# A graph layer's software pipeline re-cut: 46 steps per tile instead of 43, its small operations dealt out anew, its searches spread out

## The chip, the cores and the metric

One core of a Trainium2 chip. The metric is the device time of the whole kernel in microseconds (us). The core has a matmul engine (PE, whose weight loads stand in the profile as PEld), a vector engine (DVE), an activation engine (ACT), a general engine (POOL, which also issues indirect DMAs) and SP, which only issues DMAs. Each engine runs its own instructions in order; they meet at semaphores.

## The reference

Two graph layers run one after the other on 3327 nodes with 256 features. Layer 0 is graph attention followed by a GRU cell. The adjacency has about 4 neighbours per row.

```python
Wh = h @ W;  src = Wh @ a[:F];  dst = Wh @ a[F:]
e   = leaky_relu(src + dst.T, 0.2)
att = softmax(where(adj > 0, e, -9e15), axis=1)
gi  = (att @ Wh) @ w_ih.T + b_ih;   gh = h @ w_hh.T + b_hh
r, z = sigmoid(i_r + h_r), sigmoid(i_z + h_z);  n = tanh(i_n + r * h_n)
x = layernorm(x + (1 - z) * n + z * h)
# layer 1: two propagation steps (sparse mean, and top-p attention over all nodes),
# a sum of projections, layer norm, residual, layer norm
```

The change touches layer 0 alone.

## The kernel before

The 3327 rows are 26 tiles of 128 rows (the last has 127). Layer 0 has three kinds of work.

*Projection* (`project`, lines 743 to 759). For each tile PE transposes x (`px`), ACT copies it to `xT`, PE multiplies it with W (`pw`), ACT copies the result to one of six `table` buffers, POOL takes two columns from it (`ds`), and a DMA from ACT's queue writes it to `whx` in DRAM, from where all tiles' neighbour rows are gathered later. No gather can start before the whole of `whx` is written.

*Search* (`neighbours`, lines 809 to 828). The adjacency tile (1.66 MB, one of three buffers) comes by `load_adj` on SP's queue. DVE finds the ones in each of four segments (L814, FIND_INDEX8) and sorts the finds into a list of up to 16 neighbours (L819 to L827). These are five steps; `find()` makes one of them. At the end of a search, the load of the tile three further on is issued into the buffer that has come free.

*Tile* (`tile`, lines 830 to 1003). From the list of neighbours come the 640 edge places of the tile: `deg`, `d16`, `pst`, `half`, `square`, `mid`, `first`, `y`, `mem`, `pe`, `ei`, then `edge`, then five gathers of 128 rows from `whx` into `g` (L609, POOL). The weights of the edges are `e` (DVE) and its exponential (ACT). Five 128x128 matrices `m` carry each edge's weight in the column of its row: two are made on ACT (Square, then Relu), two on POOL and one on DVE (L936). PE multiplies them with `g` into `acc` (L942). The rest is the GRU: `prz` and `pn` get their x part (L954, L955), `h` is `acc` scaled, `ph` and `hT` turn it, L967 and L971 add its part, and `rz`, `n`, `x1`, the layer norm (`mv`, `shift`, POOL) and the q and k rows of layer 1 (`qk`) follow.

A tile is a generator, and `yield from to(s)` moves it on to its step s. The order on PE, ACT, DVE and POOL is the order in which the program issues (a manual schedule); SP's DMAs only follow their semaphores. `advance()` is one phase: it makes one `find()`, opens a new tile in every sixth phase, moves each open tile on by one step, oldest first, and moves on the first logits of layer 1, which begin when the last search is done.

```python
            find()
            if phase % EVERY == 0 and phase // EVERY < NT:
                tiles.append(self.tile(phase // EVERY))
            for g in list(tiles):
                if next(g, True):
```

With six phases per tile, a tile that is at step s stands beside others at steps s-6, s-12 and so on, and each engine has in a phase the work of all steps that are equal modulo 6. In the projection loop `find()` is called for each tile from the third on, and from tile 13 (`EARLY`) on each projected tile also makes a phase. Buffers that bind tiles together: three of `g`, ten of `m`, one PSUM bank each of `acc` and `prz`, two of `pn`, and two each of the tags `sm` (`pst`, `pe`, `pq`) and `tr` (`ph`, `ptq`, first logits).

## Time and profile before

| | us |
|---|---|
| median of three runs (lowest to highest) | 1891.27 (1889.89 to 1893.18) |
| profiled execution, its own time | 1886.47 |
| its span, first to last instruction | 1884.5 |
| last copy of the projection (L757) starts | 66.93 |
| first gather / fifth gather of tile 0 (L609) starts | 71.56 / 78.57 |
| fifth gather of tile 25 starts | 393.30 |
| last copy of layer 0 (L639) starts | 428.1 |

| engine | busy us over the span | share |
|---|---|---|
| PE | 1665.2 | 88% |
| PEld | 1223.3 | 65% |
| DVE | 1335.0 | 71% |
| POOL | 1174.2 | 62% |
| ACT | 997.8 | 53% |

The shares are means over stages with different limits. Layer 0 is the first 428 us of the span, the rest is layer 1. In the profile an engine's wait stands in brackets as "[idle before <-releaser]"; "issue" is an idle stretch in which the engine waited for nothing that the profile shows. The granted PE clock is either 1.0 or 0.5, and a mean over a window lies between.

### The profile page before, as it was taken

The page shows a single profiled execution, that of the slowest core. Times are in us where ns is not written, and L with a number is a line of the kernel's source. Part 1 is how long each engine was busy: PE and PEld are TensorE (multiplying, and loading weights), DVE is VectorE, ACT ScalarE, POOL GpSimd, SP SyncE. Part 2 cuts the span into 40 slices and gives each one's busy share as a digit, 9 for nine tenths or more (in the row PEclk, how much of TensorE's full clock was granted, in tenths as well). Part 3 has the DMA queues.
Part 4 walks back from the last instruction along what each step waited for, and adds up shares of the span by engine and source line. Part 5 has one row for each costly group of instructions (what it writes and reads, how often), then busy time and mean ns, then how long its engine had stood idle before and what let it go on. Part 6 is the DMA issues. An engine that isn't in the chain of part 4 may idle for free. (4 is left out here: it accounts for less than half of the span.)

```text
span 1884.5 us, 27520 instructions
## 1 busy us (share of the span) xinstructions
PE 1665.2 (88%) x8093; PEld 1223.3 (65%) x8093; DVE 1335.0 (71%) x4278; ACT 997.8 (53%) x2243; POOL 1174.2 (62%) x1881
## 2 busy tenths in 40 slices
PE   6578888987999999999996999999999988679994
PEld 4345455545677777777774777777777665568873
DVE  6789886446555566655564999999999977485872
ACT  3244445554556555555653555555555446676663
POOL 1477778847787666666654666655666573555764
PEclk9789889997999999999998999999999998889997
DMA  9766652213222111111101111111111110122330
GB/s 330 255 208 230 216 169 64 62 43 86 84 67 57 40 40 41 47 47 45 40 26 39 51 54 48 49 45 48 54 57 54 48 54 29 40 76 87 118 95 29
DMA packets 95482, 154.21 MB, mean 82 GB/s; under 512 B 16854, under 2 KB 68557, under 8 KB 95324
## 3 DMA queue, kind: packets, MB, share of 16 engines
q1 hardware_dynamic: 64906, 89.92, 14.5%
q0 software_dynamic: 20384, 53.28, 10.7%
q10 hardware_dynamic: 10034, 9.18, 1.5%
q8 instruction: 66, 1.08, 0.2%
q14 instruction: 92, 0.75, 0.1%
HBM read 124.65 MB, written 27.75 MB: 81 GB/s over the span
## 5 line engine op out<-in xcount | busy, mean ns | idle before, releaser
L1416 PE MATMUL pav<-xa,at 128*128 128x256 f32 (+2 forms) x1352 | 331.7, 390 | 9.0 <-ACT at L1402 8.8
L1416 PE MATMUL pav<-x,at 128*128 128x256 f32 (+2 forms) x1352 | 325.7, 385 | 7.6 <-ACT at L1402 7.6
L1402 ACT COPY at<-pt 128x512 f32<-128x512 f32 (+2 forms) x364 | 191.8, 541 | 261.8 <-PE pt L1400 260.5
L1416 PEld LDWEIGHTS pav<-xa,at 128*128 128x128 f32 (+2 forms) x1352 | 246.4, 191 | 90.0 <-ACT at L1402 43.1
L1416 PEld LDWEIGHTS pav<-x,at 128*128 128x128 f32 (+2 forms) x1352 | 244.4, 190 | 72.4 <-ACT at L1402 29.9
L1196 ACT COPY array<-pl 128x416 f32<-128x416 f32 (+4 forms) x405 | 183.2, 503 | 180.3 <-PE pl L1193 180.2
L1209 DVE MAX8 cand<-array 128x8 f32<-128x167 f32 (+5 forms) x921 | 239.0, 335 | 44.7 <-ACT array L1196 44.6
L609 POOL DMA_INDIRECT g<-xf_rows,edge x130 | 136.3, 1049 | 158.0 <-PE pxf L1362 125.6
L609 POOL DMA_INDIRECT g<-x_rows,edge x130 | 140.3, 1079 | 104.4 <-PE ptq L622 71.3
L1193 PE MATMUL pl<-kT,qT 64*128 64x416 f32 (+4 forms) x810 | 198.1, 560 | 4.5 <-ACT x L1581 2.7
L1301 DVE TENSOR_TENSOR_SCAN before<-e 128x40 f32<-128x40 f32 (+3 forms) x52 | 14.9, 286 | 225.5 <-ACT e L1294 225.5
L1354 POOL TENSOR_SCALAR m<-col,erow 128x128 f32<-128x128 f32 x260 | 162.6, 639 | 14.5 <-PE pxf L1362 8.0
L609 POOL DMA_INDIRECT g<-whx,edge x130 | 137.4, 1057 | 46.4 <-issue 32.1
L1362 PE MATMUL pxf<-g,m 128*128 128x256 f32 (+1 forms) x520 | 133.5, 406 | 15.3 <-POOL m L1354 8.6
L1362 PEld LDWEIGHTS pxf<-g,m 128*128 128x128 f32 (+1 forms) x520 | 99.0, 199 | 69.8 <-issue 41.3
L1227 DVE MAX8 lst<-cand 128x8 f32<-128x160 f32 (+3 forms) x364 | 114.6, 315 | 9.0
L1400 PE MATMUL pt<-ident,array 128*128 128x128 f32 (+1 forms) x676 | 100.9, 276 | 7.1 <-DVE array L1317 7.1
L814 DVE FIND_INDEX8 at<-ones,array 128x8 uint32<-128x840 f32 (+1 forms) x104 | 106.5, 1026 | 0.0
L1400 PE MATMUL pt<-ident,p 128*128 128x128 f32 (+2 forms) x676 | 100.2, 274 | 3.9 <-DVE p L1317 3.9
L1400 PEld LDWEIGHTS pt<-ident,array 128*128 128x128 f32 (+1 forms) x676 | 84.8, 144 | 24.8 <-PE pxf L1362 7.9
L967 PE MATMUL prz<-wih,hT 128*128 128x512 f32 (+1 forms) x104 | 67.0, 778 | 36.9 <-ACT hT L965 36.9
L1400 PEld LDWEIGHTS pt<-ident,p 128*128 128x128 f32 (+2 forms) x676 | 84.5, 144 | 21.3 <-PE pxf L1362 7.7
(473 smaller groups left out, 3369.4 us busy)
## 6 DMA issues: line engine op xcount, KB each, us to landing
array<-in_adj_dram SPq DMA_DIRECT2D x25, 1248.0 KB, 7.0
array<-in_adj_dram SPq DMA_DIRECT2D x25, 415.5 KB, 6.2
xf_rows<-xf SPq DMA_DIRECT2D x50, 128.0 KB, 1.7
xa_rows<-xa SPq DMA_DIRECT2D x50, 128.0 KB, 1.7
xfs<-xf_rows SPq DMA_DIRECT2D x50, 128.0 KB, 2.4
whx<-table ACTq DMA_DIRECT2D x25, 129.5 KB, 6.2
x_rows<-x ACTq DMA_DIRECT2D x25, 128.0 KB, 2.4
xb_rows<-xb SPq DMA_DIRECT2D x25, 128.0 KB, 1.7
```

Of the source, the lines that this page charges most:

```text
L609: self.nc.gpsimd.indirect_dma_start(out=dst[:, b, :], out_offset=None, in_=table[:, :], in_offset=bass.IndirectOffsetOnAxis(ap=self.edge[: ...
L814: nc.vector.max_index(at[:r, g, :], self.ones8[:r], ad[:r, g, :])
L967: nc.tensor.matmul(prz[:r], hT[:, c, :r], self.wih[:, c, : 2 * D], start=False, stop=(c == DC - 1))
L1193: nc.tensor.matmul(pl[:r, :w], q[on], self.sh.kT[on, n, s : s + w], start=True, stop=True)
L1196: nc.scalar.copy(l[:r, h * HALF + s : h * HALF + s + w], pl[:r, :w])
L1209: self.nc.vector.max(cand[:r, g * 8 : g * 8 + 8], src[:r, g * group : min(N, (g + 1) * group)])
L1227: nc.vector.max(lst[:r, k : k + 8], cand[:r])
L1354: nc.gpsimd.tensor_scalar(v.m[:, b, :], sh.col1, sh.erow[:, v.at, b : b + 1], None, ALU.is_equal)
L1362: nc.tensor.matmul(acc[:r, :D], v.m[:, b, :r], v.g[:, b, :], start=(b == 0), stop=(b == EB - 1))
L1400: nc.tensor.transpose(pt[: rows(j), j - j0, :r], v.p[:r, cols(j)], self.ident[:r, :r])
L1402: nc.scalar.copy(at[:, :full, :r], pt[:, :full, :r])
L1416: nc.tensor.matmul(v.acc[: v.r, :D], at[:k, j - 4 * g, : v.r], V[:k, j, :], start=(j == 0), stop=(j == NT - 1))
```

## The change

Step numbers are new throughout; a tile has 46 steps instead of 43, still six phases per tile. Where a result went from one engine to the next in the same step or in the next one, there is now mostly a step or two between. `e` is made at step 22 after gathers at 14 to 17 (before: 18, after 13 to 15); `hT` is at 31 and its matmuls at 33 and 34 (before: both at 28); the x part of `pn` is at 29 and that of `prz` at 30.

Between engines: `d1`, `d16`, the floor of `info` and `edge` go from DVE to POOL; `mid` and `first` go from DVE to ACT, `y` stays on ACT and comes two steps earlier; all five `m` are made on ACT by a Square and an Exp with the weight as its bias, so that POOL's two and DVE's one, `we`, `wm` and `minus` go; `most` is a second row of `e`.

Searches: in the projection loop `find()` is called from tile 5 on and in two of three phases (16 calls instead of 24), then once per phase up to phase 23, then five times in six phases. Only adjacency tile 0 is loaded at the start; tiles 1 and 2 are loaded from ACT's queue after projected tiles 4 and 10, and the two GRU weights after tiles 15 and 17 (before: both after 6). `a` is laid out by the host so that each partition reads 16 bytes in a row.

```diff
+FINDS = (0, 0, 0, 2, 1, 2)
+FAR = 10000.0
...
         if apart:
             yield
+            yield
         for half in (on, other):
...
-        nc.scalar.dma_start(self.a_sb, a.rearrange("(c p) o -> p (c o)", p=P))
+        nc.scalar.dma_start(self.a_sb, a)
...
-        nc.vector.tensor_scalar(info[:r, 0:1], info[:r, 0:1], 1.0, None, ALU.max)
+        yield from to(1)
+        d1 = self.small("d1", f"d1_{t}")
...
+        nc.gpsimd.tensor_scalar(d1[:r], deg[:r], 1.0, None, ALU.max)
         d16 = self.small("d16", f"d16_{t}", dtype=BF16)
-        nc.vector.tensor_scalar(d16[:r], deg[:r], 1.0, None, ALU.max)
+        nc.gpsimd.tensor_copy(d16, d1)
+        nc.gpsimd.tensor_scalar(info[:r, 0:1], info[:r, 0:1], 1.0, None, ALU.max)
         yield from to(2)
...
-        nc.gpsimd.tensor_copy(d1, d16)
...
         yield from to(4)
-        nc.vector.tensor_scalar(mid, pst[:, 0:1], -1.0, half, ALU.mult, ALU.add)
-        nc.vector.tensor_copy(first, pst[:, 0:1])
-        yield from to(6)
+        nc.scalar.activation(mid, pst[:, 0:1], AF.Identity, bias=half, scale=-1.0)
+        nc.scalar.copy(first, pst[:, 0:1])
         y = self.work.tile([P, EB * P], F32, tag="y", name=f"y{t}", bufs=1)
         nc.scalar.activation(y, self.place, AF.Square, bias=mid)
+        yield from to(6)
...
-        nc.vector.tensor_scalar(sh.edge[:, t, :], k, -1.0, float(N + 1), ALU.mult, ALU.add)
-        yield from to(13)
-        sh.gather(g, sh.whx, t, (0, 1))
-        yield from to(14)
-        sh.gather(g, sh.whx, t, (2, 3))
-        yield from to(15)
+        yield from to(14)
+        nc.gpsimd.tensor_scalar(sh.edge[:, t, :], k, -1.0, float(N + 1), ALU.mult, ALU.add)
+        sh.gather(g, sh.whx, t, (0,))
+        yield from to(15)
+        sh.gather(g, sh.whx, t, (1,))
+        yield from to(16)
+        sh.gather(g, sh.whx, t, (2, 3))
+        yield from to(17)
         sh.gather(g, sh.whx, t, (4,))
...
-        for k in (3, 4):
-            nc.scalar.activation(ms[k], sh.col1, AF.Square, bias=minus[:, k : k + 1])
-        yield from to(18)
+        for step, ks in ((20, (0, 1)), (21, (2, 3, 4))):
+            yield from to(step)
+            for k in ks:
+                nc.scalar.activation(ms[k], sh.col1, AF.Square, bias=self.erow(t)[:, k : k + 1], scale=-1.0)
+        yield from to(22)
...
-            nc.scalar.activation(ms[k], ms[k], AF.Relu, scale=v[:, k : k + 1], bias=w[:, k : k + 1])
-        yield from to(21)
-        for k in (0, 1, 2):
-            (nc.vector if k == 0 else nc.gpsimd).tensor_scalar(
-                ms[k], sh.col1, self.erow(t)[:, k : k + 1], w[:, k : k + 1], ALU.is_equal, ALU.mult
-            )
-        yield from to(24)
+        for step, ks in ((23, (0, 1)), (24, (2, 3)), (25, (4,))):
+            yield from to(step)
+            for k in ks:
+                nc.scalar.activation(ms[k], ms[k], AF.Exp, bias=e[:, 0, k : k + 1], scale=-FAR)
+        yield from to(26)
         acc = self.ps1.tile([P, 512], F32, tag="acc", name=f"acc{t}")
...
-        yield from to(25)
+        yield from to(28)
         rs = self.small("rs", f"rs{t}")
...
-        prz = self.ps1.tile([P, 2 * D], F32, tag="prz", name=f"prz{t}")
+        yield from to(29)
+        h = self.work.tile([P, D], F32, tag="h", name=f"h{t}")
+        nc.scalar.activation(h[:r], acc[:r, :D], AF.Copy, scale=rs[:r])
         pn = self.ps.tile([P, 2 * D], F32, tag="pn", name=f"pn{t}")
         ones3 = self.ones3[:, :r]
+        nc.tensor.matmul(pn[:r], ones3, self.bias[:, 2 * D :], start=True, stop=False)
+        xs = [self.xT[:, c, cols(t)] for c in range(DC)]
+        for c in range(DC):
+            nc.tensor.matmul(pn[:r, :D], xs[c], self.whh[:, c, 2 * D :], start=False, stop=False)
+        yield from to(30)
+        prz = self.ps1.tile([P, 2 * D], F32, tag="prz", name=f"prz{t}")
         nc.tensor.matmul(prz[:r], ones3, self.bias[:, : 2 * D], start=True, stop=False)
-        nc.tensor.matmul(pn[:r], ones3, self.bias[:, 2 * D :], start=True, stop=False)
...
-        yield from to(28)
+        yield from to(31)
         hT = self.work.tile([P, DC, P], F32, tag="hT", name=f"hT{t}")
         nc.scalar.copy(hT[:, :, :r], ph[:, :, :r])
+        yield from to(33)
...
+        yield from to(34)
...
-        yield from to(29)
+        yield from to(35)
 
         rz = self.work.tile([P, 2 * D], F32, tag="rz", name=f"rz{t}")
         nc.scalar.activation(rz[:r], prz[:r], AF.Tanh, scale=0.5)
-        yield from to(32)
+        yield from to(36)
...
-        yield from to(33)
+        yield from to(37)
         nc.scalar.activation(n[:r], n[:r], AF.Tanh)
-        yield from to(35)
+        yield from to(38)
...
-        yield from to(37)
+        yield from to(39)
...
-        yield from to(38)
+        yield from to(40)
         nc.scalar.activation(x1, x1, AF.Identity, bias=shift[:r], scale=mv[:r, 1:2])
         move_rows(nc.scalar, sh.x1_rows[t * P : t * P + r, :], x1, r)
-        yield from to(39)
+        yield from to(41)
         yield from sh.qk(self.ps, self.work, 0, t, x1, "tr")
...
-        for t in range(3):
-            self.load_adj(t)
+        self.load_adj(0, nc.sync)
-        cuts = (0, 8, 16, 23, NT)
+        cuts = (0, 8, 16, NT - 2, NT)
...
-                if t == 6:
-                    for w, src in zip((self.whh, self.wih), self.gates):
-                        nc.scalar.dma_start(w, src.rearrange("(c p) d -> p c d", p=P))
+                if t in (4, 10):
+                    self.load_adj(1 + t // 10, nc.scalar)
+                if t in (15, 17):
+                    w, src = ((self.whh, self.wih)[t // 17], self.gates[t // 17])
+                    nc.scalar.dma_start(w, src.rearrange("(c p) d -> p c d", p=P))
...
-                    advance()
-                elif t >= 2:
+                    advance(min(1, phase % 3))
+                elif t >= EARLY - 8:
                     find()
...
             while phase < EVERY * NT or tiles:
-                advance()
+                advance(1 if phase < 4 * EVERY else FINDS[phase % EVERY])
```

## The prediction

> **What bounds the kernel now.** Only layer 0 changes, and there the page's slices show no engine at nine tenths throughout. I therefore cut the span into stretches first, and then read what each engine waits for, and one engine's timeline.
>
> Busy time by stretch, for ten tiles (tiles 7 to 16 open at 133.4 and 266.6) and for one tile:
>
> ```profile
> core 0: us, PE busy (x) PEld busy (x) DVE busy (x) ACT busy (x) POOL busy (x), PEclk, DMA share, GB/s
> 133.40:266.60 133.20, 109.15 (x479) 67.75 (x478) 113.51 (x429) 61.46 (x190) 101.13 (x192) 0.91 0.67 216
> ```
> ```profile
> 290.15:302.25 12.10, 9.90 (x46) 6.03 (x45) 9.71 (x43) 6.71 (x22) 9.90 (x20) 1.00 0.26 67
> ```
>
> Ten tiles take 133.2 us, 13.3 each, where an undisturbed tile takes 12.1. By busy time PE, DVE and POOL are level and all about a fifth idle. The timeline of POOL over that tile says otherwise:
>
> ```profile
> 290.15 1.14 POOL L609 DMA_INDIRECT g<-whx,edge  x1 [0.52 <-PE acc L942]
> 291.59 1.00 POOL L609 DMA_INDIRECT g<-whx,edge  x1 [0.30 <-issue]
> ...
> 295.20 0.19 POOL L859 CAST d<-d 128x1 f32<-128x1 bf16 x1
> 295.49 0.18 POOL L862 TENSOR_SCALAR half<-d 128x1 f32<-128x1 f32 x1
> 295.65 0.26 POOL L864 TENSOR_SCALAR square<-d 128x1 f32<-128x1 f32 x1
> 295.85 0.19 POOL L865 CAST tell<-info 128x16 bf16<-128x16 f32 x1
> 296.13 0.25 POOL L866 TENSOR_TENSOR tell<-info,tell 128x16 bf16<-128x16 f32 x1
> 296.37 1.60 POOL L936 TENSOR_SCALAR m<-col,erow,we 128x128 f32<-128x128 f32 x2
> 298.13 1.32 POOL L609 DMA_INDIRECT g<-whx,edge  x1 [0.17 <-issue]
> ...
> 301.47 0.26 POOL L998 TENSOR_SCALAR shift<-mv 128x1 f32<-128x1 f32 x1
> 302.25 1.13 POOL L609 DMA_INDIRECT g<-whx,edge  x1 [0.52 <-PE acc L942]
> ```
>
> There is no real wait in it. Every gather carries a gap of 0.30 after another gather, 0.17 after `m` and about 0.5 after a small operation, whichever releaser is named; the small ones stand 0.16 to 0.29 apart although they last 0.19. POOL is full: 12.1 us is its own work. The fifth gather of tile 0 starts at 78.57, that of tile 25 at 393.30: 25 intervals of 12.59. So POOL's work makes 12.1 of it and waits the rest. From the waits at 120 to 290 us (total, times, longest):
>
> ```profile
> PEld prz L967 <- ACT hT L965: 24.6, 13, 2.7
> DVE e L922 <- DMA g<-whx,edge: 15.7, 5, 5.2
> POOL g L609 <- issue: 15.0, 54, 0.5
> POOL mv L995 <- DVE which L894: 10.2, 6, 2.0
> ```
>
> POOL's one true wait is `mv`, 2 us in about every second tile: DVE sits in `e` for a gather that has not landed (landing takes 2.7 to 9.0 us, while adjacency loads keep the DMA share at 0.67), makes up its queue, and reaches the layer norm late. PE's wait for `hT`, 1.9 per tile, is beside POOL's chain.
>
> The projection (to 66.93) is another regime. Its waits:
>
> ```profile
> PE pa L737 <- DMA a_sb<-in_a_dram: 9.9, 1, 9.9
> DVE at L814 <- DMA array<-in_adj_dram: 9.6, 3, 6.1
> ACT xT L749 <- DMA whx<-table: 4.9, 2, 2.8
> ```
>
> The DMA share is 0.95 over the first 70 us (327 GB/s): x, the rows of `whx`, the GRU weights and eight adjacency tiles compete.
>
> **The sum for before**, in trace time: 67 projection, 11.6 to tile 0's fifth gather, 314.7 for 25 intervals, 34.8 from there to the end of layer 0 at 428, and 1456.4 of layer 1: 1884.5. The profiled execution has 1886.5 with what lies around the span; the median of the runs is 1891.3, 4.8 above. I put savings to the median as they come out.
>
> **Part 1, POOL's period.** Out: both `m`, 296.37 to 298.13, 1.76. The lone gather then follows a small operation instead of `m`: +0.33. The cast of `d` goes, -0.29; `d1`, `d16` and the floor of `info` come, by the spacing of `half`, `square`, `tell`: 0.28+0.28+0.18 = +0.74. `edge` comes with an output in uint32 that POOL shows nowhere: between 0.16 (the spacing of a small operation) and 0.5, taken at 0.25, as DVE needs 0.17 for it and POOL 0.21 to 0.32 for other 128x5 operations. New period 12.10-1.76+0.33-0.29+0.74+0.25 = 11.37, that is -0.73, over 25 intervals **-18**.
>
> A rule speaks against this move: the Trainium skill, "GPSIMD Engine Reference", section "Engine selection", wants elementwise work on VectorE[...]. The rows: `d` on DVE lasts 0.146, a cast of the same size on POOL 0.19 to 0.22, but what counts on a full POOL is its spacing.[...] I keep the rows.
>
> **Part 2, POOL's waits.** The 25 intervals exceed 12.1 by more than 0.5 each; the first two (10.7, 11.0) and last two (10.8, 10.5) are short of work, so the other 21 carry 271.7-254.1 = 17.6 of waiting. `e` is now five steps behind the last gather instead of three: at 1.9 us per step 9.5 us instead of 6.3, at the upper end of landing. I keep a quarter of the wait: **-13**. What is late next: `edge` (step 14) and `mv` (39) wait for DVE one step earlier. DVE's work per tile is 11.35 with 1.2 searches; 0.2 of a search less (a segment search is 1.03, the sort about 1, so 5.1 each) is -1.0, and `info`, `d16`, `mid`, `first`, `edge`, `most` and one `m` (0.15+0.15+0.20+0.15+0.17+0.16+0.33) is -1.3: 9.0. It has room of 2.4.
>
> **Part 3, ACT and PE.** ACT loses two Square, two Relu, `we`, `wm`, `minus` (6.8+8.8 over 20 each: 1.5, plus 0.6), gains five Square and five Exp, `mid` and `first`. Exp with a bias column has no row of this size; Square with one is 0.386, Relu with two 0.486, both are the bounds, I take 0.386: 3.9+0.35. 6.15 rises to about 8.3, under 11.4: cost nothing, covered by POOL. If that cover went, ACT would be due at 8.6, the `x_rows` issue of 0.33 included. Moved past ACT's queue is also `mid`, which waits for POOL's `half`; behind it stand `y`, `rz`, `h`. PE's `hT` stall goes (two steps lie between), which leaves 9.9 per tile: no gain in time, as POOL holds the period. Its only effect is on the clock, which was 0.91 here; at 10 of 11.4 it should be nearer 1.
>
> **Part 4, projection.** In a clean stretch (19.51, 20.60, 21.93, 23.02) a tile costs ACT 1.17: 26 make 30.4 from 12.3. Before, 0.9 of weight issues and 1.5 of tile work come to it: 45, so 22 of the 67 are stalls. Afterwards: start about 2 earlier, as `a` comes in 128 runs instead of 512 (between 0 and 3.6: it takes 8.0 to land, the bigger W2 4.4); four adjacency issues on ACT's queue, each like the GRU weights' 0.4 to 0.5, +1.8; two tiles' `mid`, `first`, +1.5. SP's queue is relieved of four issues. Stalls: adjacency traffic falls from eight loads to about six, 3.3 MB, at 395 GB/s 8 us; DVE, in whose queue the searches stood, makes 16 instead of 24, and its 9.6 us on `array` mostly go. On the other side, writes of `whx` now queue behind 1.66 MB on the same queue, twice 4 us, with six `table` buffers (7 us) to absorb it. I take 9 of stalls left of 22. Sum -2+1.8+1.5-13 = about **-12**, between -21 and 0.
>
> **Part 5, the end.** After the last gather there are 28 steps instead of 27 at 1.29 each: **+1.5**. The last search ends near phase 148 instead of 119; first logits still end with the last tile, since their chunks wait for finished tiles: 0. Layer 1 is untouched: 0.
>
> **Sum**: -18-13-12+1.5 = -41.5. Smaller POOL contention (the cast took 0.45 once beside a DVE search) and the last intervals, from which 0.74 more goes, add about -3. Forecast 1891-45 = **1846**.
>
> **The rivals.**
> R1, POOL is not the bound, busy time is right. The skill's "Perfetto Trace Analysis", section "Identifying the Most-Contended Engine", takes occupancy for GPSIMD and LDWEIGHTS busy time for TensorE. By it POOL's 9.9 of 12.1 has room, LDWEIGHTS has 6.0, and with the stall at `hT` gone the period falls to PE's 9.9 plus hops, 10.3: -57-12+1.5, 1824. The gapless timeline speaks against it, the unexplained gaps "issue" for it. Chance 0.13.
> R2, new waits in the place of the old: the period stays at 12.1 (ACT's `x` and `mid` wait for POOL, and `rz`, which frees the single `prz` bank, stands behind). -12-12+1.5: 1869. The 17.6 us of waits show that such loops exist; the longer distances speak against. Chance 0.18.
> R3, the projection gains nothing, as its writes stand behind adjacency loads in one queue: 1858. Chance 0.06.
> R4, slower. The one mechanism: ACT blocked at `mid` or `x` behind a full POOL holds `rz`, PE stops at `prz` long enough each tile for its clock to fall, and PE becomes the bound. It decides from a mean interval of 12.59+12/25 = 13.1 on; with 1 us of idle PE that needs 9.9 of work at a clock of 0.82. At 13.6 the sum is +25-12 = +13, 1904. The window 133 to 267 had 0.91 at 13.3, so it is not absurd; chance 0.05.
> The forecast keeps 0.58. The kernel does what it says in the order of its instructions, so nothing is kept for that.
>
> **How the numbers follow.** The forecast's own range is 1832 to 1860 (stalls of the projection 9 either way, `edge` 7, waits 6). To leave out no more than two in ten the range must take in R1 and R2: 1820 to 1870. This kernel's runs spread so that about 0.2% (3.8 us) can be told from no change. Faster 0.94 (all but R4 and a sliver of R2), same 0.01, slower 0.05.
>
> **What would show it.** Right: POOL in mid layer 0 without a true wait and with 11.2 to 11.6 between fifth gathers; no `mv` wait; `e` not waiting for `g`; PE without the wait for `hT`; last copy of the projection at 50 to 58; layer 0 over at about 383. Wrong: POOL waiting for DVE or ACT in every tile (R2), a period under 11 (R1), a clock below 0.85 in mid layer 0 (R4).

## The result and the profile after

The kernel after takes 1860.93 us (median; 1859.89 to 1862.4), the kernel before in the same session 1890.62: ratio 0.984, interval 0.9824 to 0.9858, 29.7 us. Its profiled execution has 1861.15 with a span of 1859.1. The forecast was 1846, in a range of 1820 to 1870: faster, as said, but with two thirds of the gain. Set beside the terms of the prediction, in trace time:

| term | before | after | predicted change | measured |
|---|---|---|---|---|
| start of tile 0's fifth gather | 78.57 | 76.17 | -12 | -2.4 |
| the 25 intervals between fifth gathers | 314.7 | 284.9 | -34 | -29.8 |
| last fifth gather to the end of layer 0 | 34.8 | 38.7 | +1.5 | +3.9 |
| layer 1 | 1456.4 | 1459.3 | 0 | +2.9 |

The sum is -25.4 (1884.5 to 1859.1); the profiled execution before was some 4 us quicker than the median of its runs, which is the rest. Layer 1 isn't touched by the change; in the profiled executions of this study it took from 1453 to 1464, so below the stages of layer 0 are compared in the traces, and whole times by their ratios to the kernel before, with intervals.

The windows of the kernel after, ten tiles and one tile (from fifth gather to fifth gather), in the columns of the rows of before:

```profile
128.44:245.86 117.42, 107.26 (x470) 65.36 (x468) 98.51 (x330) 74.41 (x241) 94.78 (x201) 0.91 0.65 214
199.30:211.05 11.75, 11.75 (x47) 7.34 (x47) 9.96 (x33) 7.46 (x26) 9.46 (x20) 0.79 0.67 212
```

Ten tiles in 117.4 where there were 133.2, and each takes 11.7 or 11.8: the irregular intervals (12 to 15 us) have gone. PE's clock is 0.91 as before. In the one tile PE shows busy throughout, at a clock of 0.79, and ten tiles have it busy for nine tenths: that PE is the bound is a rival to be tested below. POOL's timeline over the same tile:

```profile
199.30 1.01 POOL L613 DMA_INDIRECT g<-whx,edge  x1 [0.30 <-issue]
200.33 0.21 POOL L918 TENSOR_TENSOR src<-ei 128x5 f32<-128x5 f32 x1
200.65 0.76 POOL L921 TENSOR_SCALAR e<-src,dmax 128x5 f32<-128x5 f32 x1
201.38 0.43 POOL L880 CAST tell<-info 128x1 bf16<-128x1 f32 x1
201.89 0.19 POOL L881 TENSOR_TENSOR tell<-info,tell 128x1 bf16<-128x1 f32 x1
202.05 0.23 POOL L858 TENSOR_SCALAR d<-deg 128x1 f32<-128x1 f32 x1
202.34 0.19 POOL L860 CAST d<-d 128x1 bf16<-128x1 f32 x1
202.49 0.21 POOL L862 TENSOR_SCALAR info<-info 128x1 f32<-128x1 f32 x1
202.78 0.20 POOL L908 TENSOR_SCALAR edge<-k 128x5 uint32<-128x5 f32 x1
203.26 1.15 POOL L613 DMA_INDIRECT g<-whx,edge  x1 [0.28 <-POOL edge L908]
...
207.01 1.11 POOL L613 DMA_INDIRECT g<-whx,edge  x1 [0.43 <-issue]
...
211.05 1.01 POOL L613 DMA_INDIRECT g<-whx,edge  x1 [0.31 <-issue]
```

Again no true wait. `d`, its cast and the floor of `info` take 0.73 from start to start (202.05 to 202.78; forecast 0.74). What the forecast didn't have is in two rows: `e`'s second row with 0.76, where the same addition as `most` lasted 0.32 before, and the cast of `tell` with 0.43, 0.18 before. The two in the undisturbed tile of before:

```profile
299.81 0.32 POOL L915 TENSOR_SCALAR most<-src,dmax 128x5 f32<-128x5 f32 x1
300.08 0.18 POOL L874 CAST tell<-info 128x1 bf16<-128x1 f32 x1
```

DVE in the tile of after, at that moment:

```profile
200.42 0.55 DVE L884 TENSOR_SCALAR mem<-y,square 128x640 bf16<-128x640 f32 x1
200.88 0.42 DVE L989 SCALAR_TENSOR_TENSOR n<-rz,n 128x256 f32<-128x256 f32 x1
201.33 0.42 DVE L990 TENSOR_TENSOR x<-x,n 128x256 f32<-128x256 f32 x1
```

POOL's `e` starts beside `mem` and ends 0.11 after the end of `n`; the cast of `tell` starts beside `x` and ends 0.06 after it. And the waits at 120 to 290 us (total, times, longest):

```profile
ACT x L1001 <- POOL shift L999: 40.2, 15, 3.6
POOL g L613 <- issue: 18.8, 57, 0.4
...
ACT hT L964 <- PE ph L961: 14.5, 10, 3.2
```

The three true waits of before (`prz` for `hT`, `e` for `g`, `mv` for DVE) are gone; POOL's only entries are the gaps ahead of its gathers. ACT now waits for POOL's `shift`, some 2.7 us in nearly every tile, at its instruction `x`; nothing that POOL needs comes late by it, as POOL has no wait.

### The profile page after: what moved, and what is told of

Read it like the earlier page. It is cut to its first block, busy times and chain, and to the rows that moved or that the text cites. A ratio compares the mean times of both kernels' runs of the same rounds, so it can differ in the third digit from the quotient of the medians.

```text
span 1859.1 us, 27521 instructions
## 1 busy us (share of the span) xinstructions
PE 1666.4 (90%) x8093; PEld 1221.4 (66%) x8093; DVE 1318.3 (71%) x4095; ACT 1031.2 (55%) x2373; POOL 1158.7 (62%) x1908
## 5 line engine op out<-in xcount | busy, mean ns | idle before, releaser
L613 POOL DMA_INDIRECT g<-x_rows,edge x130 | 146.1, 1124 | 103.6 <-PE ptq L626 70.9
L1357 POOL TENSOR_SCALAR m<-col,erow 128x128 f32<-128x128 f32 x260 | 157.0, 618 | 14.4 <-PE pxf L1365 8.0
L1320 DVE SCALAR_TENSOR_TENSOR array<-array,t,array 128x3327 f32<-128x3327 f32 x26 | 96.2, 3699 | 0.5
```

Of the source, the lines that this page charges most:

```text
L613: self.nc.gpsimd.indirect_dma_start(out=dst[:, b, :], out_offset=None, in_=table[:, :], in_offset=bass.IndirectOffsetOnAxis(ap=self.edge[: ...
L1320: nc.vector.scalar_tensor_tensor(v.p[:r], v.l[:r, :N], v.t[:r], v.p[:r], ALU.is_ge, ALU.mult, accum_out=sA[:r])
L1357: nc.gpsimd.tensor_scalar(v.m[:, b, :], sh.col1, sh.erow[:, v.at, b : b + 1], None, ALU.is_equal)
```

## The experiments

The theory to test: POOL's own queue sets layer 0's period; new steps took its waits away, `m` on ACT lowered its floor, and part was given back by small operations and by what DVE does beside them. Rivals: PE and ACT in their order set the period; or one part of the change alone made the gain; and for the projection, that the volume of DMA sets its end, not the order in ACT's queue. The experiments have the numbers that the texts of the expectations use; there is no 3 and no 5. The period is the usual interval between fifth gathers in the middle of layer 0, each trace is of one execution, and each ratio is to the kernel before in the same session.

| | median us, ratio to before (interval) | fifth gather of tile 0 | steady period | 25 intervals | end of layer 0 |
|---|---|---|---|---|---|
| before | 1890.6 | 78.57 | 12.1 and waits | 314.7 | 428.1 |
| after | 1860.9, 0.9841 (0.9824 to 0.9858) | 76.17 | 11.75 | 284.9 | 399.8 |
| 4: before, `m` on ACT | 1887.6, 0.9996 (0.9983 to 1.0009) | 78.25 | irregular | 307.2 | 428.3 |
| 6: after, with POOL's work of before | 1881.3, 0.9975 (0.9965 to 0.9985) | 76.06 | 12.80 | 310.8 | 423.9 |
| 1: small operations on DVE | 1842.4, 0.9756 (0.9721 to 0.9791) | 74.77 | 11.08 | 271.2 | 384.6 |
| 8: as 1, one row of `e` later | 1838.2, 0.9732 (0.9716 to 0.9748) | 75.69 | 10.72 | 263.1 | 377.4 |
| 11: after, one row of `e` later | 1845.5, 0.9777 (0.9753 to 0.9801) | 75.35 | 10.93 | 269.6 | 383.6 |
| 7: as 1 and 2, that row on ACT | 1858.6, 0.9834 (0.9818 to 0.9851) | 75.60 | 11.6 | 285.6 | 399.1 |
| 9: as 7, adjacency loads on SP | 1860.9, 0.9836 (0.9817 to 0.9855) | 76.00 | 11.6 | 284.2 | 398.6 |
| 2: after, adjacency loads on POOL's queue | 1854.8, 0.9833 (0.9804 to 0.9863) | 71.42 | 11.72 | 286.6 | 396.7 |
| 10: after, searches at the old pace | 1862.7, 0.9852 (0.9835 to 0.9869) | 82.68 | 11.1 to 11.8 | 281.1 | 403.9 |
| 12: as 8, loads off ACT's queue | 1844.1, 0.9771 (0.9748 to 0.9793) | 72.39 | 10.72 | 264.4 | 375.4 |
| 13: as 12, `d1`, `d16`, `info` on POOL | 1847.3, 0.9782 (0.9758 to 0.9806) | 74.35 | 10.8 | 269.2 | 382.2 |
| 14: as 8, `edge` on POOL | 1836.7, 0.9747 (0.9727 to 0.9768) | 76.11 | 10.93 | 265.5 | 380.2 |

### 4 and 6: `m` alone, and the change without POOL's part

The kernel before with this edit:

```diff
-        for k in (3, 4):
+        for k in range(EB):
             nc.scalar.activation(ms[k], sh.col1, AF.Square, bias=minus[:, k : k + 1])
...
-        for k in (3, 4):
+        for k in range(EB):
             nc.scalar.activation(ms[k], ms[k], AF.Relu, scale=v[:, k : k + 1], bias=w[:, k : k + 1])
...
-        for k in (0, 1, 2):
-            (nc.vector if k == 0 else nc.gpsimd).tensor_scalar(
```

> The kernel before with one part of the change alone: all five m made on ACT (Square then Relu), so POOL loses its two and DVE its one; steps, searches and small operations as before. POOL loses 1.43 us per tile (1.76 out, 0.33 more gap). Theory in its strong form (POOL alone sets the period of 12.1): the undisturbed period falls to 10.7 and 25 intervals by up to 35 us, with the waits for late gathers kept about -20 to -30 against before. Rival (re-stepping is what matters, since the short steps between ACT and PE and the wait for mv hold at 12): 25 intervals fall by less than 8 us. Slower is possible if ACT, with 9 us of work per tile in the old short steps, holds hT up: +5 to +15.

No change: 0.9996. POOL has 1.43 less per tile and the intervals fall by 7.5 only, which the tail takes back (42.8 instead of 34.8). The waits at 120 to 290 us of this kernel:

```profile
ACT rz L973 <- PE prz L963: 33.1, 13, 3.4
PEld prz L963 <- ACT hT L961: 28.4, 14, 2.8
POOL mv L991 <- DVE which L894: 18.5, 13, 2.1
```

POOL waits for `mv` in nearly every tile instead of in every second one: what POOL no longer does, it waits. The strong form of the theory, POOL alone, falls for the kernel before.

The kernel after with POOL's load of before. New steps, the new pace of searches, the new loads and `mid` and `first` on ACT stay, so it is more than the steps alone:

```diff
-        for step, ks in ((20, (0, 1)), (21, (2, 3, 4))):
+        for step, ks in ((20, (3,)), (21, (4,))):
...
-        for step, ks in ((23, (0, 1)), (24, (2, 3)), (25, (4,))):
-            yield from to(step)
-            for k in ks:
-                nc.scalar.activation(ms[k], ms[k], AF.Exp, bias=e[:, 0, k : k + 1], scale=-FAR)
+        yield from to(23)
+        w = self.small("we", f"we{t}", EB)
+        nc.scalar.activation(w, e[:, 0, :], AF.Exp)
+        for k in (3, 4):
+            nc.scalar.activation(ms[k], ms[k], AF.Exp, bias=e[:, 0, k : k + 1], scale=-FAR)
+        yield from to(24)
+        for k in (0, 1, 2):
+            (nc.vector if k == 0 else nc.gpsimd).tensor_scalar(
...
```

and `d1`, `d16`, the floor of `info` and `edge` on DVE, as in experiment 1.

> The kernel after with POOL's load as before: new steps and searches, but d1/d16, the floor of info and edge on DVE, and m made as before (two on POOL, one on DVE, two on ACT). Theory (POOL's queue is the bound): POOL has its 12.1 us per tile again, with no waits; 25 intervals of about 12.0 to 12.2 instead of 12.6 before and 11.4 after, so about +12 to +20 us against after and -10 to -17 against before. Rival (only the new steps matter): the same time as after within 3 us. Rival (only the m on ACT matter): the same as before in the intervals, about +30 us against after.

The waits are gone, as predicted, and every interval in the middle is 12.8. But 12.8 is more than the undisturbed 12.1 of before, with the same instructions on POOL. Its timeline (`L938` is `m`, `L919` the second row of `e`):

```profile
198.38 0.21 POOL L916 TENSOR_TENSOR src<-ei 128x5 f32<-128x5 f32 x1
198.69 0.71 POOL L919 TENSOR_SCALAR e<-src,dmax 128x5 f32<-128x5 f32 x1
199.40 1.81 POOL L938 TENSOR_SCALAR m<-col,erow,we 128x128 f32<-128x128 f32 x2
201.16 0.18 POOL L878 CAST tell<-info 128x1 bf16<-128x1 f32 x1
```

`e` has 0.71 instead of 0.32 and the pair of `m` 1.81 instead of 1.60; at 198.41 DVE starts `mem` and then `n` and `x`. From start to start, `e` takes 0.44 more than in the undisturbed tile of before. The pair of `m` takes 1.76 in both, but there it stood ahead of a gather, with a gap of 0.17; here it stands ahead of `tell`, and the gather behind `tell` has a gap of 0.60. The gathers and the other gaps are some 0.35 shorter. So the kernel loses 17.6 us of waits and gets 0.7 per tile back, some 14.7 over 21 steady intervals; in all the intervals fall by 3.9 us. Neither part is worth more than 0.3% alone; together, without the small operations, they are worth 2.4% (experiment 1).

### 1: the small operations back on DVE

```diff
-        yield from to(1)
-        d1 = self.small("d1", f"d1_{t}")
...
-        nc.gpsimd.tensor_scalar(d1[:r], deg[:r], 1.0, None, ALU.max)
-        nc.gpsimd.tensor_copy(d16, d1)
-        nc.gpsimd.tensor_scalar(info[:r, 0:1], info[:r, 0:1], 1.0, None, ALU.max)
+        nc.vector.tensor_scalar(info[:r, 0:1], info[:r, 0:1], 1.0, None, ALU.max)
+        nc.vector.tensor_scalar(d16[:r], deg[:r], 1.0, None, ALU.max)
...
+        nc.gpsimd.tensor_copy(d1, d16)
...
+        nc.vector.tensor_scalar(sh.edge[:, t, :], k, -1.0, float(N + 1), ALU.mult, ALU.add)
         yield from to(14)
-        nc.gpsimd.tensor_scalar(sh.edge[:, t, :], k, -1.0, float(N + 1), ALU.mult, ALU.add)
```

> The kernel after with d1/d16, the floor of info and edge back on DVE, as they were before; steps, searches and the five m on ACT stay. POOL loses about 0.75 us per tile (0.99 in, 0.29 for the cast of d back). Theory (POOL's own instruction queue sets the tile period, 11.75 us in the steady state): the period falls to about 11.0, over some 21 steady tiles and the rest about -15 to -19 us against the kernel after. Rival (PE and ACT in their fixed order set the period, POOL only fills it): period stays 11.7, time within 3 us. Rival (DVE is as near to its limit): DVE gains 0.7 us per tile, edge waits behind DVE's queue, 0 to +6 us.

The period goes from 11.75 to 11.08, the intervals from 284.9 to 271.2, the ratio from 0.984 to 0.976: POOL's queue is what binds, and these four operations cost 0.67 per tile there (forecast: 0.74+0.25-0.29 = 0.70). Both rivals fall: PE and ACT have the same work and the same order, and DVE has more work. POOL and DVE at one tile of this kernel:

```profile
193.14 0.63 POOL L919 TENSOR_SCALAR e<-src,dmax 128x5 f32<-128x5 f32 x1
193.75 0.30 POOL L878 CAST tell<-info 128x1 bf16<-128x1 f32 x1
194.13 0.38 POOL L879 TENSOR_TENSOR tell<-info,tell 128x1 bf16<-128x1 f32 x1
```
```profile
193.12 0.55 DVE L882 TENSOR_SCALAR mem<-y,square 128x640 bf16<-128x640 f32 x1
193.59 0.42 DVE L987 SCALAR_TENSOR_TENSOR n<-rz,n 128x256 f32<-128x256 f32 x1
194.04 0.43 DVE L988 TENSOR_TENSOR x<-x,n 128x256 f32<-128x256 f32 x1
```

Each of POOL's three ends 0.04 to 0.10 after one of DVE's three: `e` (193.77) after `mem` (193.67), the cast (194.05) after `n` (194.01), the subtraction (194.51) after `x` (194.47). In the first three tiles of the same kernel, where DVE stands in FIND_INDEX8 at that moment, `e` lasts 0.31 to 0.34. DVE's own three have the same means here and in the eighth kernel, where they lie beside other work (0.55, 0.42, 0.43): only POOL pays.

The fourteen traces, from 70 to 400 us, say it over many rows. A row of POOL that started while DVE was in `mem` was over 0.06 longer than the shortest of its kind in 90% of 199 cases, in `x<-x,n` in 84% of 177, and in FIND_INDEX8 in none of 1394. It was in none of 25 in `n<-n,pn`, which does the same kind of work as `n<-rz,n` (84% of 109) but has its second input in PSUM. So among DVE's longer instructions it does not count that DVE is busy, but whether it reads two inputs from SBUF, or is `mem`.

### 8 and 11: one instruction four steps later

```diff
         e = self.st.tile([P, 2, EB], F32, tag="e", name=f"e{t}", bufs=3)
-        nc.gpsimd.tensor_scalar(e[:, 1, :], src, self.dmax, None, ALU.add)
...
         for step, ks in ((20, (0, 1)), (21, (2, 3, 4))):
             yield from to(step)
+            if step == 21:
+                nc.gpsimd.tensor_scalar(e[:, 1, :], src, self.dmax, None, ALU.add)
```

> The first experiment with one instruction moved: POOL's second row of e is made at step 21, where DVE stands in a search, instead of step 17, where it lay beside DVE's mem (f32 to bf16) and lasted 0.63. Same instructions on every engine. Theory (the two engines hold each other up, so the duration depends on what stands beside it): the instruction falls to 0.31 to 0.34 as in the first three tiles beside FIND_INDEX8; the period falls by 0.31 less 0.14 of a longer gap ahead of the next gather, to about 10.9. Rival (its duration is its own in this program, from its operands' places): 0.63 still, and the period rises to about 11.2.

In experiment 1's kernel: the row falls from 0.63 to 0.33, both operations of `tell` to 0.18 and 0.19, and the period from 11.08 to 10.72, more than expected. The row does not lie beside a search, as expected, but beside the short operations of DVE's sort. POOL's timeline:

```profile
200.18 0.25 POOL L916 TENSOR_TENSOR src<-ei 128x5 f32<-128x5 f32 x1
200.38 0.18 POOL L878 CAST tell<-info 128x1 bf16<-128x1 f32 x1
200.65 0.19 POOL L879 TENSOR_TENSOR tell<-info,tell 128x1 bf16<-128x1 f32 x1
201.88 1.08 POOL L613 DMA_INDIRECT g<-whx,edge  x1 [1.04 <-DVE mem L882]
...
205.06 0.28 POOL L998 TENSOR_SCALAR shift<-mv 128x1 f32<-128x1 f32 x1
205.31 0.33 POOL L924 TENSOR_SCALAR e<-src,dmax 128x5 f32<-128x5 f32 x1
205.82 1.15 POOL L613 DMA_INDIRECT g<-whx,edge  x1 [0.19 <-issue]
```

Two things are to be seen. The row is nearly free where it is now: from `shift` to the gather are 0.76 with it, and 0.69 in the kernel after without it (206.32 to 207.01), since it lies in the gap that a gather has after a small operation anyway. And POOL now has a true wait: 1.04 ahead of the first gather instead of some 0.4. The profile names `mem`; what the gather reads is DVE's `edge`, just ahead of it, which ended at 201.13. DVE has no idle stretch of 0.15 or more between 150 and 290 us in this trace: with POOL relieved, DVE reads as the next bound, at 10.72 per tile. That is read from the trace; experiments 13 and 14 take work off DVE, but load POOL by it.

> The kernel after with only POOL's second row of e moved from step 17 to step 21, where DVE stands in a search. Theory (of the 11.75 per tile 0.4 to 0.6 is POOL's small operations held up by what DVE does beside them: the second row 0.76 instead of 0.33, the cast of tell 0.43 instead of 0.19): both fall to 0.33 and 0.19, the period to 11.2 to 11.3, near the 11.37 of the forecast, and about -10 us in the 25 intervals against after. Rival (the eighth run's gain came from DVE's relief, not from POOL's): DVE has room here, so the period stays within 0.1 of 11.75.

The same edit in the kernel after itself, with all small operations left on POOL: 11.75 to 10.93, 15.3 us in the intervals, ratio 0.978. The row lasts 0.33; the cast of `tell` still has 0.45, now beside `mem`. So the sum of the prediction, 11.37 by POOL's undisturbed rows, is beaten once one row stands elsewhere: its collision is out, and it lies in a gap besides. The rival (the gain was DVE's relief) falls, as DVE has room here and the period moved all the same. So does PE as the bound: no instruction of PE moved in experiments 1 and 11, and the period fell by 0.67 and 0.82.

### 7 and 9: the same row on ACT instead

```diff
-        nc.gpsimd.tensor_scalar(e[:, 1, :], src, self.dmax, None, ALU.add)
+        yield from to(18)
+        nc.scalar.activation(e[:, 1, :], src, AF.Identity, bias=self.dmax)
```

> The first experiment (small operations back on DVE) and the second (adjacency loads 1 and 2 on POOL's queue) together, and e's second row on ACT (Identity with dmax as bias, step 18) instead of POOL. POOL loses another 0.63 + 0.1 per tile, to a floor of about 10.3. Theory (POOL full at 11.07, but DVE next: in a tile of the first experiment DVE had 0.22 us of idle in 11.08): the period falls to 10.8 to 10.9 and DVE's queue becomes the gapless one; about -5 in the intervals and -3 to -5 from the projection against the first experiment, ratio to before about 0.971. Rival (POOL alone counts): 10.3, -19 in the intervals. Rival (PE with 10.3 of work at a clock of 0.96 is already the bound): period stays at 11.07.

A miss of all three expectations: the row has left POOL and the period rises from 11.08 to 11.6. ACT, then POOL:

```profile
199.90 0.30 ACT L920 ACTIVATE e<-src,dmax 128x5 f32<-128x5 f32 x1 [1.28 <-issue]
200.10 0.22 ACT L891 COPY ei<-pe 128x100 f32<-128x100 f32 x1
```
```profile
199.65 0.21 POOL L916 TENSOR_TENSOR src<-ei 128x5 f32<-128x5 f32 x1
199.80 0.19 POOL L878 CAST tell<-info 128x1 bf16<-128x1 f32 x1
200.07 0.19 POOL L879 TENSOR_TENSOR tell<-info,tell 128x1 bf16<-128x1 f32 x1
202.31 1.06 POOL L613 DMA_INDIRECT g<-whx,edge  x1 [2.05 <-DVE mem L882]
```
```profile
200.36 0.17 DVE L896 TENSOR_TENSOR which<-place,ei 128x5 f32<-128x5 f32 x1 [0.85 <-ACT ei L891]
201.39 0.17 DVE L905 TENSOR_SCALAR edge<-k 128x5 uint32<-128x5 f32 x1
```

ACT stands at the row for 1.28 until POOL has made `src` (the profile names nothing, but `src` ends 0.04 before); behind it waits `ei` of the next tile, whose list DVE needs for `edge`, which POOL's next gather needs: POOL, ACT, DVE (which waits 0.85 for `ei`), POOL, with a wait of 2.05 at the end. The row on POOL waited for nobody, since `src` stands ahead of it in the same queue. This is the mechanism of the prediction's R4 (ACT blocked behind POOL), by another instruction.

The ninth run has the same edit and all three first adjacency loads on SP at the start:

```diff
-        self.load_adj(0, nc.sync)
+        for t in range(3):
+            self.load_adj(t, nc.sync)
...
-                if t in (4, 10):
-                    self.load_adj(1 + t // 10, nc.scalar)
```

> As the seventh, but all three first adjacency loads are issued at the start from SP's queue, as before the change. Theory (whx's writes must not stand behind an adjacency load in one queue; the early volume costs little): ACT's stalls on whx<-table stay away and the last projection copy comes near 58, as with POOL's queue. Rival (volume: 5 MB beside x and the weights in the first 20 us): the first transposes wait for x, the last copy comes at 61 to 65, and the time is 3 to 6 us over the seventh.

Ratio 0.9836 (0.9817 to 0.9855), last copy at 62.4, tile 0's fifth gather at 76.00: the place of these two loads makes no difference against the seventh (62.83, 75.60). The theory's 58 did not come; the last copy lies where the rival had it, and the time is 2.3 over the seventh's, within the noise.

### 2, 10 and 12: the projection

```diff
-                    self.load_adj(1 + t // 10, nc.scalar)
+                    self.load_adj(1 + t // 10, nc.gpsimd)
```

> The kernel after with the loads of adjacency tiles 1 and 2 issued from POOL's queue instead of ACT's; nothing else. Theory (the writes of whx stood behind 1.66 MB loads in ACT's queue, two stalls of 3.9 and 3.7 us): both stalls at xT go, the last projection copy comes 4 to 7 us earlier than 62.9 and the time falls by 4 to 6 us. Rival (the volume moved through the DMA engines sets the end of the projection, in whichever queue it stands): the stalls move to other transfers, last copy within 2 us of 62.9, time within 2 us.

Last copy at 58.16, first gather 64.77 instead of 69.51: 4.7, as the theory said, although one of the two stalls stays (4.6 at `xT`, for an adjacency load). The whole (0.9833, 0.9804 to 0.9863) does not show it. In the trace one gather in the middle came late, and an interval of 14.1 stands among those of 11.7. In the kernel after the two stalls were these, on ACT's timeline:

```profile
34.26 0.37 ACT L754 COPY xT<-px 128x256 f32<-128x256 f32 x1 [3.88 <-DMA whx<-table]
38.62 0.37 ACT L754 COPY xT<-px 128x256 f32<-128x256 f32 x1 [3.71 <-DMA array<-in_adj_dram]
```

The twelfth takes the GRU weights off ACT's queue as well, in the kernel of the eighth:

```diff
-                    nc.scalar.dma_start(w, src.rearrange("(c p) d -> p c d", p=P))
+                    nc.gpsimd.dma_start(w, src.rearrange("(c p) d -> p c d", p=P))
```

> The eighth with nothing but the writes of whx left on ACT's queue while projecting: adjacency loads 1 and 2 and both GRU weights are issued from POOL's queue. Theory (writes behind loads in one queue stall the table buffers): no wait of ACT for whx<-table, last projection copy at 55 to 58 instead of 62.9, -4 to -7 against the eighth. Rival (DMA volume): the waits only change names (for adjacency, for weights), last copy 60 to 63 as in the seventh and ninth, time within 2 us of the eighth.

Between the two theories: last copy at 59.62, fifth gather 3.3 earlier than in the eighth, 3.5 us of short waits for `whx<-table` and one of 4.1 for an adjacency load left; ratio 0.9771 (0.9748 to 0.9793), not better than the eighth, again with one gather late. The thirteenth, with the same loads as the twelfth, has its last copy at 61.85. The seventh, with loads 1 and 2 on POOL's queue too, got nothing (fifth gather at 75.60, against 74.77 in experiment 1), and has a wait of 4.5 for `whx<-table` later. So the order in ACT's queue costs between nothing and 4.7 us; more these runs don't settle.

The tenth is the kernel after with this edit:

```diff
-                    advance(min(1, phase % 3))
-                elif t >= EARLY - 8:
+                    advance(1)
+                elif t >= 2:
...
-                advance(1 if phase < 4 * EVERY else FINDS[phase % EVERY])
+                advance(1)
```

> The kernel after with the searches at the old pace: one in every phase and from projected tile 2 on, the rest unchanged (loads 1 and 2 on ACT's queue, small operations on POOL). DVE has 1.0 us more per tile until the searches are done, about 10 of 11.75. Theory (POOL bound; the prediction's part on DVE's room was right): period within 0.15 of 11.75 while searches last, less afterwards, as they end sooner; projection 2 to 5 us longer, from 24 searches instead of 16 and more adjacency traffic; time +2 to +5 against after. Rival (the fewer searches were what removed the waits): waits of POOL for DVE return, period 12 to 12.6, +8 to +20.

With the searches at their old pace the fifth gather of tile 0 comes at 82.68, 6.5 later than in the kernel after and 4.1 later than before the change, and the intervals have 281.1, 3.8 less. DVE's waits for adjacency are 15.1 instead of 6.7, ACT's for `whx<-table` 9.3 instead of 6.0. POOL waits for DVE in one tile of the middle alone (1.0 and 1.2 us, an interval of 13.6): fewer searches are not what removed the waits of before. The period is not the 11.75 expected, but mostly 11.1 to 11.4 while the searches last (to 267) and 11.7 to 11.9 afterwards, the other way round than expected. POOL's `e` lasts 0.33 in most of its tiles and 0.76 at most: with more searches DVE stands elsewhere at that moment. The new pace is worth 6.5 in the projection and gives 3.8 back; what else changed up to that point costs some 4.

### 13 and 14: back towards balance

The twelfth, with

```diff
-        nc.vector.tensor_scalar(info[:r, 0:1], info[:r, 0:1], 1.0, None, ALU.max)
-        nc.vector.tensor_scalar(d16[:r], deg[:r], 1.0, None, ALU.max)
+        nc.gpsimd.tensor_scalar(d1[:r], deg[:r], 1.0, None, ALU.max)
+        nc.gpsimd.tensor_copy(d16, d1)
+        nc.gpsimd.tensor_scalar(info[:r, 0:1], info[:r, 0:1], 1.0, None, ALU.max)
...
-        nc.gpsimd.tensor_copy(d1, d16)
```

> As the twelfth, with d1, d16 and the floor of info on POOL as after has them (edge stays on DVE). In the eighth POOL waits about 0.8 us per tile for DVE's edge in a period of 10.71, so DVE is the bound there; this takes 0.2 to 0.3 us from DVE and gives POOL 0.45. Theory (balance of the two): period 10.4 to 10.5, -5 to -7 us in the intervals against the twelfth. Rivals: PE at 10.1 of work per tile is the bound, period within 0.1 of 10.71; or POOL is the bound again at once (more of its operations beside DVE's), 10.9 to 11.2, +5 to +12.

Period 10.8, ratio 0.9782 (0.9758 to 0.9806), no gain. On POOL `d` and its cast last 0.39 and 0.34 here, beside DVE's `n` and `x`, where they had 0.23 and 0.19 in the kernel after. By its number this is as near to the rival with PE (within 0.1 of 10.71) as to the last outcome named, POOL as the bound at once. The trace speaks for POOL: between 130 and 300 us its queue has no gap over 0.6 but for one late gather.

And the eighth, with

```diff
-        nc.vector.tensor_scalar(sh.edge[:, t, :], k, -1.0, float(N + 1), ALU.mult, ALU.add)
         yield from to(14)
+        nc.gpsimd.tensor_scalar(sh.edge[:, t, :], k, -1.0, float(N + 1), ALU.mult, ALU.add)
```

> The eighth with edge on POOL, as after has it; d1, d16 and the floor of info stay on DVE. So of the change's moves of small operations to POOL only edge is kept, and the second row of e stands at step 21. POOL's floor by the eleventh (10.93 with all of them) less 0.45 for the d operations: 10.5; DVE's by the eighth (10.71, bound by it) less 0.2: 10.5. Theory (the two queues bound the period, whichever is longer): 10.5, about -5 us in the intervals against the eighth, ratio to before about 0.970. Rivals: PE's 10.1 of work with its hops holds 10.7; or edge after k costs a hop ahead of the first gather (0.3 to 0.5) that the eighth doesn't have, 10.7 to 11.0 and up to +6 us.

10.93 instead of the 10.5 expected, 2.4 more in the intervals than the eighth, ratio 0.9747 (0.9727 to 0.9768), not told apart from the eighth's. It is in the range of the second rival, a hop behind `k`, but POOL has no wait for `k` there: its gathers have their usual gaps, and its rows are longer. The collision has wandered on, to `src` and both of `tell`:

```profile
202.01 0.56 POOL L916 TENSOR_TENSOR src<-ei 128x5 f32<-128x5 f32 x1
202.53 0.37 POOL L878 CAST tell<-info 128x1 bf16<-128x1 f32 x1
202.98 0.39 POOL L879 TENSOR_TENSOR tell<-info,tell 128x1 bf16<-128x1 f32 x1
```

The eighth, 1838.2 and 0.9732, is the quickest of these kernels by its ratio, though not clear of the first and the fourteenth, and its interval lies below that of the kernel after.

## Why the prediction was right, and where it was off

**What bounds the kernel** was right: POOL's own list, at four fifths of busy time. Experiment 11 shows it in the kernel after (one instruction moved on POOL alone, 0.82 per tile), experiment 1 for the small operations. R1 (occupancy) falls for this kernel: at 9.46 busy of 11.75 POOL was full. In the eighth, at 10.72, DVE seems to bind. R2 (new waits) falls by the list of waits: POOL has none. Of R4 the blocked ACT was there (`x`, 2.7 us for `shift`), but it held up nothing that POOL waits for, and PE's clock was 0.91 over ten tiles, though 0.79 in the one shown; R3's mechanism was there, in part.

**Part 1**, 12.10 to 11.37, came out at 11.75. Its terms can now be read one by one:

| step | forecast | measured |
|---|---|---|
| all but POOL's part (before's clean tile, 6) | 0 | +0.70 |
| `m` to ACT (6, 1) | -1.43 | -1.72 |
| `d`, `d16`, `info`, `edge` to POOL (1, after) | +0.70 | +0.67 |
| sum | -0.73 | -0.35 |

The split over the rows depends on the order of the experiments: the forecast's +0.33 for the gap ahead of the gather falls into the first row, since in experiment 6 `m` no longer stands ahead of a gather, and so `m` gave back nearly its full 1.76. The price of the moved operations was right. The spacing of `half`, `square` and `tell` in the lines shown is 0.16, 0.20 and 0.28, which makes 0.64 and not 0.74; that 0.73 came was in part luck.

Set side by side, start to start, the clean tile of before and the tile shown of after differ from the forecast by this: `e` +0.46, the cast of `tell` +0.23, three more small rows +0.08, and on the other side some -0.4 of shorter gathers and gaps. So the step that failed is one that wasn't there: the durations on POOL were taken as fixed, while re-cut steps set POOL's small operations beside other ones of DVE. The forecast had seen such a case and misread it. It names a cast of 0.45 "beside a DVE search" and books the way out of it as a small gain; in the trace the cast starts beside `x`, ends 0.04 after it, and the search comes behind:

```profile
282.83 0.45 POOL L859 CAST d<-d 128x1 f32<-128x1 bf16 x1
```
```profile
282.82 0.42 DVE L984 SCALAR_TENSOR_TENSOR x<-rz,x 128x256 f32<-128x256 f32 x1
283.23 1.03 DVE L814 FIND_INDEX8 at<-ones,array 128x8 uint32<-128x840 f32 x1
```

A rule would have told the side: the Trainium skill, "SBUF — State Buffer", section "Who interferes with whom", has DVE and GpSimd share a port pair as an exclusive lock; a DVE instruction with two SBUF inputs contends by it with a GpSimd instruction that reads SBUF, and one in a two-port mode holds the pair for its whole length. The rows fit: POOL's operations end 0.04 to 0.11 after DVE's `mem`, `n` or `x`, and neither FIND_INDEX8, with one input, nor `n<-n,pn`, with one of its two in SBUF, costs POOL anything. By the page the order of issue decides who is blocked; here that is not seen. Where POOL's operation came first and `mem`, `n` or `x` started with at least 0.1 of it to go, DVE's was over 0.05 longer in 1 of 120 cases of the fourteen traces. That the port is the cause is the page's; the runs show that the neighbour on DVE is.

**Part 2**, -13 for the waits: they went entirely (-17.6), and `e` waits for `g` no longer (not once between 120 and 290 us). But experiment 6 shows that this and the new 0.7 per tile come together: the two make -3.9.

**Part 3**: cost nothing, as said; POOL has no wait for ACT, and `prz` none for `hT`. The clock did not go nearer to 1: 0.91 over ten tiles, as before. It is 0.99 over the same stretch in the eighth, with shorter tiles; what sets it was not tried. ACT's cover is thinner than the sum of its work said: 0.3 us of work in the wrong place (experiment 7) costs 0.5 per tile.

**Part 4**, -12, is the term that failed by most: -2.4. The start came 1.2 earlier instead of 2. Fewer searches brought their share (6.5 by experiment 10). The stalls, put at 9, are about 16 in the trace: from the first `xT` at 11.1 to the last copy are 51.8, less the clean 30.4 and the 5.7 of issues and tile work that the prediction lists. The largest are the two of 3.9 and 3.7 for `whx<-table` and `array`, which the prediction named and set off against six buffers. And between the last copy and the first gather there are 6.6 us instead of 4.6: POOL's `edge` waits 3.8 for DVE's `k`, a wait that experiment 1 only moves (4.9, POOL's gather for DVE's `edge`). Why the stalls stayed is open in part: experiments 2, 7, 12 and 13 move the loads off ACT's queue and get between 4.7 us and nothing.

**Part 5**, +1.5, was +3.9. The tail of the kernels with the new steps has 37 to 40. The steps there are longer than the 1.29 assumed (`hT` waits up to 3.2 for `ph`, which now stands behind `prz`'s x part on PE); this was read, not tried.

**Sum**: -45 forecast, -29.7 measured: 10 too much in the projection, 4 too much in the period and waits together, 2 too little in the tail and 3 in layer 1, against which stand the 4 by which the profiled execution before was quicker than its median. The forecast's own range, 1832 to 1860, was just missed. The time lies in the part of the wider range that was there for R2, whose mechanism did not come, so that it lies within 1820 to 1870 is in part luck. The signs named beforehand came out so: no `mv` wait, no wait of `e`, none for `hT`; but the period not in 11.2 to 11.6, the last copy at 62.9 instead of 50 to 58, the end of layer 0 at 399.8 instead of 383.

## What to carry to other kernels

When an in-order engine is full, price a moved instruction by the spacing of its neighbours, and then look at what stands beside it on the other engines. Here that was DVE beside POOL: the same addition lasted 0.33 or 0.76 by its place alone, and moving it by four steps took 15.3 us out of the intervals, where the whole change took 29.8. Two bounds that hold at the same number (a full queue and a loop of waits) must be taken away together; either alone measured as nothing or next to nothing. An instruction whose input comes from the full engine can be better off on that engine, behind its producer: on ACT, with its input from POOL, it blocked a queue and cost 0.5 per tile.

## What the hardware showed beyond that

- POOL's small operations lasted 0.18 to 0.33 alone (`mv`'s power, 0.58, is the exception), and 0.30 to 0.76 where they met DVE's `mem` (f32 to bf16) or one of its operations with two inputs in SBUF. DVE's durations hardly change: the medians of `mem` and `x` are 0.58 and 0.45 in experiment 11 and 0.53 to 0.55 and 0.42 to 0.43 in the others.
- A gather starts 0.30 after a gather, 0.42 to 0.44 after `shift`, and 0.28 after `edge`. The row of `e`, put between `shift` and the gather, costs 0.07 instead of its 0.33; the gap behind it is 0.19.
- In the profiled executions of experiments 2, 7, 12 and 13, which are all those with loads on POOL's queue, one gather in the last third of layer 0 came late: after a gap of 2.6 to 2.8 us instead of 0.3 (in the seventh 4.6 instead of 2.0), so that its interval was 2.4 to 2.9 longer. In the other kernels none did at that place. What it is stays open.
